# Four layers on one core: where the exponentials of the last layer stand, how its last tiles are read out, and where a flag is loaded

## The chip, the core and the metric

The kernel runs on one core of a Trainium2 chip. A core has five engines with a queue of instructions each, which they work off in order: TensorE (matmul), VectorE, ScalarE, GpSimd and SyncE; in the profile they are PE (with PEld for its weight loads), DVE, ACT, POOL and SP. They wait for each other by semaphores only. Data move between main memory and the on-chip memory by DMA, and TensorE writes into a small memory of its own, PSUM, which VectorE and ScalarE can read. The metric is device time in microseconds. A time is the median of runs without the profiler; one further execution was taken by the hardware profiler, and all views of the trace come from it.

## The reference, cut to what matters

Four layers follow each other on x of shape (4, 512, 32, 32), each as `x = x + layer(groupnorm(x))`. The first three (attention over pixels with mixed heads, a gate, a second attention) are not touched by the change. The last one looks up rows of a pool of 2048 items:

```python
q = jnp.transpose(x, (0, 2, 3, 1)).reshape(-1, C)          # 4096 tokens x 512
att = q @ mempool.T                                         # 4096 x 2048
vals, idx = jax.lax.top_k(att, k)                           # k = 8
vals = jax.nn.softmax(vals, axis=1)
att_sparse = jnp.zeros_like(att).at[rows, idx].set(vals)
out = att_sparse @ mempool                                  # a weighted sum of 8 rows
```

So for each token the eight best of 2048 scores are found, their softmax is taken, and the eight items are added with these weights.

## The kernel before

All lines are of the kernel before. `fast_net` (line 42) computes all four layers; while it does, it keeps sums from which a check can tell whether the softmaxes of the earlier layers, which are taken without a maximum, stayed in range. `check_range` (L2017) turns them into one number, `flag`. `nc.values_load(flag)` puts it into a register of every engine, which is one instruction in each of the five queues, and at the very end the program branches on it to a slower general version (L2788), which isn't run here.

The last layer cuts the 4096 tokens into 32 tiles of 128. For each tile:

- TensorE multiplies the tile's tokens by the pool. Tiles 2 to 29 go in pairs (`two_tiles`, L1568), by a scheme of seven products of half size in the place of eight. A product is four matmuls of 128x128 by 128x512 in float32, which the profile shows as eight instructions of line L1596. The first, second, third and seventh products are copied out of PSUM by ScalarE (L1600); the others are added to scores that are there by VectorE (L1050, `att<-att,pair`). The third, fifth and seventh products go on adding to PSUM in which the first stood, and the fourth to that of the second, so each of these begins after the copy of what stands there. Tiles 0, 1, 30 and 31 are multiplied in the plain way (`attention`, L1522; matmuls L1531, copies L1536), the last one in three parts.
- `pick` (L1609): VectorE finds the eight largest scores (L1620; for the last tile from three partial maxima, L1617 and L1618) and their indices (L1622); GpSimd sends eight indirect DMAs, which gather a row of 512 for each token (L1625); VectorE negates the largest score (L1631), and ScalarE takes the exponentials with their sum (L1634, two instructions). SyncE loads the tile of x that the result is added to (L1636).
- `ready` (L1664): VectorE inverts the sum (L1668) and ScalarE scales the exponentials to weights (L1669). `weigh_rows` (L1671): ScalarE scales the eight gathered rows, one instruction each (L1674). `add_up` (L1677): VectorE adds the rows in a tree of three additions of 1024 and one of 512 (L1050, `got` and `acc`). `turn_back` (L1685): TensorE transposes the sum in four pieces (L1689). `put` (L1692): VectorE adds x (L1695) and SyncE stores the tile (L1696).

The last tiles have a second way: `weigh` (L1639) makes weights on VectorE, `diagonals` (L1644) lets ScalarE write eight diagonal matrices of the weights (L1648), and `read_last` (L1651) lets TensorE multiply the gathered rows by them, 32 matmuls of 128x128 (64 instructions, L1657), so that weighing, adding and transposing are one accumulation in PSUM. Before, tiles 30 and 31 are read in this way, and tile 29 and all ahead of it by the tree.

The order of the work is written out by hand: `pin` keeps an instruction behind everything that was written before it for its engine. What is not pinned, such as the load of the flag, is placed by a scheduler, and what is pinned behind it goes along. The loop at L2049 runs over n = 2, 4, ... 28, one pair of tiles a pass. It draws the seven products out of `two_tiles` one by one and puts between them the picking of tiles n - 1 and n and the weighing, adding, turning and storing of tiles n - 4 to n - 1. In pass n = 12 it calls `check_range`, in pass n = 14 it loads the flag (L2073). Behind the loop, L2108 to L2145 write out the same for the last tiles: s is the tile whose scores are made.

On ScalarE the order in a pass before is: copy of the last pass's seventh product, four rows of n - 3, copy of the first product, four rows of n - 3, exponential of n - 1, copies of the second and third, weights and four rows of n - 2, weights of n - 1, four rows of n - 2, exponential of n. There are three places in PSUM for products, and three buffers for scores.

Of the kernel before, what the change touches and what calls it, by code (L numbers as in the profile page):

```python
# [16 lines left out]
P = 128  # L17
# [14 lines left out]
TOPK = 8  # L32
# [9 lines left out]
def fast_net(ctx: ExitStack, tc: tile.TileContext, a: dict, out: bass.AP, flag: bass.AP):  # L42
# [13 lines left out]
    def pin(ins):  # L56

        return tc.keep_in_program_order(ins)
# [1460 lines left out]

        return eight_k([P, NI], f"att_{n}", at)  # L1520

    def attention(n, between=None, at=None):  # L1522

        b, tt = tiles[n]
        att = new_att(n, at)
        for i, (lo, hi) in enumerate(
                ((0, T), (T, T + NB), (T + NB, NI)) if n == len(tiles) - 1 else ((0, T), (T, NI))):
            sc = flat2(next_pair())
            for i0 in range(lo, hi, NB):
                for k in range(KC):  # L1530
                    pin(nc.tensor.matmul(  # L1531
                        sc[:, i0 - lo:i0 - lo + NB],
                        xn3[b][:, k, tt * P:(tt + 1) * P], memT[k][:, i0:i0 + NB],
                        start=(k == 0), stop=(k == KC - 1),
                    ))
            pin(nc.scalar.copy(att[:, lo:hi], sc[:, 0:hi - lo]))  # L1536
            if between is not None and i == 0:
                between()
        return att

    mem_t = [eT_flat[:, i * NI:(i + 1) * NI].rearrange("p (k q) -> p k q", k=2) for i in range(4)]
# [18 lines left out]
    def token_sums(n):  # L1560

        a11, a12, a21, a22 = token_blocks(n)
        s1, s2, s3, s4 = token_places
        sub7(s3, a11, a21)
        add7(s1, a21, a22)
        sub7(s2, s1, a11)
# [42 lines left out]
    def pick(n, att):  # L1609

        b, tt = tiles[n]
        nm = f"{b}_{tt}"
        top = small.tile([P, TOPK], F32, tag="top", name=f"top_{nm}")
        if n == len(tiles) - 1:
            tops = small.tile([P, 3, TOPK], F32, tag="tops", bufs=1, name="tops")
            for i, (lo, hi) in enumerate(((0, T), (T, T + NB), (T + NB, NI))):
                pin(nc.vector.max(tops[:, i, :], att[:, lo:hi]))  # L1617
            pin(nc.vector.max(top, tops.rearrange("p i n -> p (i n)")))  # L1618
        else:
            pin(nc.vector.max(top, att))  # L1620
        ix = small.tile([P, TOPK], mybir.dt.uint32, tag="ix", name=f"ix_{nm}")
        pin(nc.vector.max_index(ix, top, att))  # L1622
        got = big("qkv"[n % 3], f"got_{nm}").rearrange("p k (i c) -> p (k i) c", c=C)
        for i in range(TOPK):
            pin(nc.gpsimd.indirect_dma_start(  # L1625
                out=got[:, i, :], out_offset=None, in_=a["mem"],
                in_offset=bass.IndirectOffsetOnAxis(ap=ix[:, i:i + 1], axis=0),
                bounds_check=NI - 1, oob_is_err=False,
            ))
        nmx = small.tile([P, 1], F32, tag="nmx", name=f"tmx_{nm}")  # L1630
        pin(nc.vector.tensor_scalar_mul(nmx, top[:, 0:1], -1.0))  # L1631
        et = small.tile([P, TOPK], F32, tag="et", name=f"et_{nm}")
        rs = small.tile([P, 1], F32, tag="rs", name=f"trs_{nm}")
        pin(nc.scalar.activation(et, top, AF.Exp, bias=nmx, scale=1.0, accum_out=rs))  # L1634
        xr = spare[:, n % 4 * NB:(n % 4 + 1) * NB].rearrange("p (k q) -> p k q", q=P)
        nc.sync.dma_start(out=xr, in_=x2[b][:, :, tt * P:(tt + 1) * P])  # L1636
        return got, et, rs, xr

    def weigh(et, rs, nm):  # L1639
        ri = small.tile([P, 1], F32, tag="ri", name=f"tri_{nm}")  # L1640
# [23 lines left out]
    def ready(n, picked):  # L1664

        got, et, rs, xr = picked
        ri = small.tile([P, 1], F32, tag="ri", name=f"tri_{n}")
        pin(nc.vector.reciprocal(ri, rs))  # L1668
        pin(nc.scalar.activation(et, et, AF.Identity, scale=ri))  # L1669

    def weigh_rows(picked, lo, hi):  # L1671
        got, et, rs, xr = picked
        for i in range(lo, hi):
            pin(nc.scalar.activation(  # L1674
                got[:, i, :], got[:, i, :], AF.Identity, scale=et[:, i:i + 1]))
# [272 lines left out]
    for b in range(B):  # L1948
        last = b + 1 == B
        behind = chain(  # L1950
            behind if b else state["behind"], norm3(b - 1) if b > 0 else gating(B - 1))
        ahead = prepare3(0) if last else prepare2(b + 1)
        if last:
            load_memory()
        for s, u in enumerate(UNITS2):
            if s == 5 and not last:
                load2(b + 1)
            if s == 5 and last:
                img[b]["Wp"] = load_w("Wp", f"Wp2_{b}")
            if s >= 1:  # L1960
                scores2(b, u, UNITS2[s - 1], last or u != UNITS2[-1])
            for _ in range(2):
                if s >= 3 and last:
                    next(behind, None)
                if s >= 7:
                    next(ahead, None)
            if s == 9 and b == 0:
                weights = weight_sums(1, "Wq")
            if s >= 10 and b == 0:
                next(weights, None)  # L1970
            if s == len(UNITS2) - 2 and not last:
                run_out(ahead)
                first7, rest7 = input_sums(img[b + 1]["xn"])
                first7[0]()
        run_out(ahead)
        if not last:
            first7[1]()
            first7[2]()
        apply2(b, UNITS2[-1])
        if last:  # L1980
            atts[0] = attention(0, lambda: invert2(b))
            finish2(b)
            put_out2(b, memory_sums())
            continue
        over_keys(b, *UNITS2[-1][:2])
        at_border[0] = True
        for i, _ in enumerate(seven_by_channels(b + 1, "q", bq2)):
            if 1 <= i < 3:
                rest7[i - 1]()
            if i == 4:  # L1990
                invert2(b)
            if i == 5 and b == 0:
                run_out(weight_sums(1, "Wk"))
            if i in (2, 3, 5, 6):
                next(behind, None)
        load_sums(b, "Wp", b == 0)
        for i, _ in enumerate(seven_by_channels(b + 1, "k", bk2)):
            if i == 1:
                finish2(b)
            if b == 0 and i == 2:  # L2000
                run_out(weight_sums(1, "Wv"))
            if b == 0 and i == 4:
                run_out(weight_sums(0, "Wp"))
            next(behind, None)
        first7, rest7 = input_sums(img[b]["o"])
        for i, _ in enumerate(seven_v(b + 1)):
            if 2 <= i < 5:
                first7[i - 2]()
            elif i >= 5:
                rest7[i - 5]()  # L2010
            next(behind, None)
        run_out(behind)
        at_border[0] = False
        scores2(b + 1, UNITS2[0])
        seven_out(b)
# [16 lines left out]

    atts[1] = attention(1)
    picks[0] = pick(0, atts.pop(0))
    token_sums(2)
    att_at[0] = (turns8[0] - 1) % 3
    made = {}

    def add_tile(n):
        made[n] = add_up(n, picks.pop(n))  # L2040

    def turn_tile(n):
        sums[n] = turn_back(n, made.pop(n))

    def put_tile(n):
        put(n, sums.pop(n))

    ahead = iter(())
    for n in range(2, end - 2, 2):  # L2049
# [19 lines left out]
        next(behind, None)  # L2069
        if n == 12:  # L2070
            check_range()
        if n == 14:
            again = nc.values_load(flag, min_val=0, max_val=1)  # L2073
        ready(n - 2, picks[n - 2])
        if n > 2:
            add_tile(n - 3)
# [18 lines left out]

        next(parts)
        atts[n + 1] = next(parts)
        if n + 2 < end - 2:
            token_sums(n + 2)
        if n > 2:  # L2100
# [7 lines left out]
        turn_tile(s - 4)  # L2108
        weigh_rows(picks[s - 3], 4, TOPK)

    atts[s] = attention(s, first_part, (att_at[0] + 1) % 3)
    picks[s - 1] = pick(s - 1, atts.pop(s - 1))
    ready(s - 2, picks[s - 2])
    put_tile(s - 4)
    add_tile(s - 3)
# [1 line left out]

    s = end - 1
    picks[s - 1] = pick(s - 1, atts.pop(s - 1))
    ready(s - 2, picks[s - 2])  # L2120

    def second_part():
        turn_tile(s - 4)
        weigh_rows(picks[s - 2], 0, 4)

    atts[s] = attention(s, second_part, (att_at[0] + 2) % 3)
    put_tile(s - 4)
    weigh(*picks[s - 1][1:3], s - 1)
    add_tile(s - 3)
    weigh_rows(picks[s - 2], 4, TOPK)  # L2130
    diags[0] = diagonals(0, picks[s - 1][1])

    s = end
    picks[s - 1] = pick(s - 1, atts.pop(s - 1))
    turn_tile(s - 4)
    weigh(*picks[s - 1][1:3], s - 1)
    add_tile(s - 3)
    put_tile(s - 4)
    turn_tile(s - 3)
    diags[1] = diagonals(1, picks[s - 1][1])  # L2140
    put_tile(s - 3)
    sums[s - 2] = read_last(picks.pop(s - 2), diags[0])
    sums[s - 1] = read_last(picks.pop(s - 1), diags[1])
    put_tile(s - 2)
    put_tile(s - 1)  # L2145
    return again


# [702 lines left out]
```

## Time and profile before

| | |
|---|---|
| median of 3 runs | 2495.71 us (2493.08 to 2501.78) |
| the profiled execution | 2504.67 us, of which the span of its instructions 2503.0 us |
| TensorE, VectorE, GpSimd, ScalarE busy | 97%, 74%, 49%, 47% of the span |
| mean granted clock of TensorE | 0.994 of full speed |
| last layer's loop, 13 passes from n = 4 | 2082.63 to 2433.74 us |
| one late pass (2366.00 to 2392.73) | 26.73 us: TensorE 25.18 busy, VectorE 24.16, GpSimd 17.19, ScalarE 15.00 |
| behind the loop (2433.74 to 2503.00) | 69.26 us: TensorE 46.49 busy, VectorE 36.91, GpSimd 34.71, ScalarE 25.95 |

How to read the lines of the profile: a row of the timeline gives the start in us from the first instruction, the duration in us, the engine, the line of the kernel, the operation, the tile written and the tiles read, sizes, and how many instructions are merged (x8). In brackets stands how long the engine was idle before it, and whose work ended that idle time; "issue" is a wait that the profile does not explain. Matmuls are pipelined, so a product's row is longer than the distance to the next one's start. A row of the waits gives a total, a count and the longest wait. A q behind the engine's name (ACTq) means its queue: an instruction that only sets or loads registers.

### The profile page before, as it was taken

To read this page: it belongs to the slowest core of one execution; us is meant where nothing else is said; L and a number is where in the kernel's file an instruction comes from. 1 tells how busy PE (TensorE), PEld (TensorE's weight loads), DVE (VectorE), ACT (ScalarE), POOL (GpSimd) and SP (SyncE) were. 2 spreads that over 40 slices of the span, in tenths; PEclk is the share of its full clock that TensorE was granted. 3 is DMA by queue.
4 is the path that set the end of the run, shared out by engine and by line. 5 is a ranking of instruction groups with operands and counts; after the bars stand their busy time and mean duration, and the time that the engine had idled before them with its cause. 6 is when DMAs were issued, how large, how long until landed. Compare 5 with 4: busy or idle time off the path is not lost. (4 is left out here: it accounts for less than half of the span.)

```text
span 2503.0 us, 47967 instructions
## 1 busy us (share of the span) xinstructions
PE 2430.2 (97%) x18400; PEld 1154.5 (46%) x18400; DVE 1847.7 (74%) x2918; ACT 1175.1 (47%) x1516; POOL 1215.8 (49%) x1688
## 2 busy tenths in 40 slices
PE   9999999999999999999999999999999999999996
PEld 4344534555355534555633633453363344444444
DVE  5799568875788548886768677576857657889894
ACT  1567346652666336651253145125324516565653
POOL 3266425553465435554284247127405616666664
PEclk9999999999999999999999999999999999999998
DMA  2588348872698438893301230131114046777765
GB/s 85 154 225 232 118 130 228 241 218 85 176 243 234 140 89 212 244 243 131 103 24 68 104 128 18 64 110 46 55 39 147 26 132 176 230 218 198 200 194 158
DMA packets 190031, 367.18 MB, mean 147 GB/s; under 512 B 32985, under 2 KB 96473, under 8 KB 185570
## 3 DMA queue, kind: packets, MB, share of 16 engines
q1 hardware_dynamic: 109712, 186.58, 23.9%
q0 software_dynamic: 49152, 142.79, 21.2%
q10 hardware_dynamic: 30930, 34.66, 5.1%
q8 instruction: 148, 2.42, 0.4%
q14 instruction: 89, 0.73, 0.1%
HBM read 190.10 MB, written 39.58 MB: 92 GB/s over the span
## 5 line engine op out<-in xcount | busy, mean ns | idle before, releaser
L552 DVE STREAM_TRANSPOSE eT<-e 128x1024 f32<-128x1024 f32 x256 | 316.6, 1237 | 197.1 <-ACT e L546 196.5
L528 POOL DMA_DIRECT2D s<-ss x512 | 258.2, 512 | 386.4 <-PE pair L539 110.5
L1365 ACT ACTIVATE eT<-pair 128x1024 f32<-128x1024 f32 x256 | 248.2, 1022 | 312.4 <-PE pair L1371 189.1
L1625 POOL DMA_INDIRECT got<-in_mem,ix x256 | 277.1, 1082 | 202.7 <-issue 68.8
L567 DVE BATCH_NORM_STATS2 st<-e 128x6 f32<-128x256 f32 x1024 | 350.8, 405 | 0.0
L546 ACT ACTIVATE e<-pair 128x1024 f32<-128x1024 f32 x256 | 250.4, 1022 | 161.7 <-PE pair L539 129.9
L1389 POOL TENSOR_TENSOR e<-eT 128x1024 f32<-128x1024 f32 x96 | 239.3, 2496 | 167.0 <-ACT eT L1365 122.0
L519 ACT COPY ss<-pair 128x1024 f32<-128x1024 f32 x256 | 247.2, 1020 | 83.7 <-PE pair L513 41.7
L513 PE MATMUL pair<-k,q 64*32 64x512 f32 x4096 | 267.3, 598 | 11.5 <-ACT e L546 11.5
L578 PEld LDWEIGHTS pv<-eT,v 128*64 128x64 f32 x4096 | 221.1, 137 | 71.6 <-issue 55.2
L578 PE MATMUL pv<-eT,v 128*64 128x128 f32 x4096 | 250.0, 275 | 4.0 <-ACT pv L638 4.0
L1371 PE MATMUL pair<-q,k 64*128 64x512 f32 x1024 | 239.9, 605 | 1.8 <-DVE sum L1050 0.9
L1390 DVE TENSOR_TENSOR eT<-eT,e 128x1024 f32<-128x1024 f32 x96 | 146.9, 1530 | 126.7 <-POOL e L1389 126.4
L1596 PE MATMUL pair<-eT,tokens 128*128 128x512 f32 x448 | 201.3, 592 | 0.0
L539 PE MATMUL pair<-s,wmix 32*32 32x512 f32 x4096 | 160.0, 599 | 3.0 <-DMA s<-ss 2.1
L1385 POOL TENSOR_TENSOR eT<-eT 128x1024 f32<-128x1024 f32 x32 | 83.0, 2593 | 161.4 <-ACT eT L1365 156.1
L1371 PEld LDWEIGHTS pair<-q,k 64*128 64x128 f32 x1024 | 92.3, 186 | 140.0 <-issue 66.6
L1674 ACT ACTIVATE got<-got,et 128x512 f32<-128x512 f32 x240 | 153.2, 711 | 1.4 <-DMA got<-in_mem,ix 1.0
L513 PEld LDWEIGHTS pair<-k,q 64*32 64x32 f32 x4096 | 57.1, 105 | 178.5 <-ACT e L546 85.4
L1050 DVE TENSOR_TENSOR k<-k,pair 128x512 f32<-128x512 f32 (+1 forms) x96 | 78.0, 857 | 73.6 <-PE pair L1123 60.5
L1596 PEld LDWEIGHTS pair<-eT,tokens 128*128 128x128 f32 x448 | 84.1, 190 | 100.9 <-issue 98.1
L651 POOL TENSOR_TENSOR o<-pv,rb 64x256 f32<-64x256 f32 x128 | 118.7, 927 | 6.3
(410 smaller groups left out, 3706.3 us busy)
## 6 DMA issues: line engine op xcount, KB each, us to landing
s<-ss SPq DMA_DIRECT2D x512, 128.0 KB
s<-ss POOLq DMA_DIRECT2D x512, 128.0 KB
rb<-r POOLq DMA_DIRECT2D x64, 128.0 KB
o<-o SPq DMA_DIRECT2D x32, 256.0 KB
xr_c<-x SPq DMA_DIRECT2D x32, 256.0 KB
rb_c<-r SPq DMA_DIRECT2D x64, 128.0 KB
e<-x SPq DMA_DIRECT2D x32, 256.0 KB
out<-e SPq DMA_DIRECT2D x32, 256.0 KB
```

The costliest lines, as they stand in the source:

```text
L513: pin(nc.tensor.matmul(sc[m * NS:(m + 1) * NS, r, :], q[r * HD:(r + 1) * HD, m, s * NS:(s + 1) * NS], k_[r * HD:(r + 1) * HD, m, n * NB:(n ...
L519: pin(nc.scalar.copy(ss[:, :, n * NB:(n + 1) * NB], sc))
L528: pin(relays[side].dma_start(out=s2[2 * m + r::NH], in_=ss[m * NS:(m + 1) * NS, r, :]))
L546: pin(nc.scalar.activation(e[:, half].rearrange("p r qq k -> p (r qq k)"), flat2(mixed(s, half)), AF.Exp))
L552: pin(nc.vector.transpose(eT[:, j % 2].rearrange("p b (qq i r) x -> p i r qq b x", qq=2, i=4)[:, i, 2 * half:2 * half + 2], e[:, half].rea ...
L567: pin(nc.vector.bn_stats(st[:, i, 2 * half + r, qq, :], e[:, half, r, qq, :]))
L578: pin(nc.tensor.matmul(pv[r * HD:(r + 1) * HD, gp, :], I["v"][:, t, g * HD:(g + 1) * HD], eT[:, j % 2, t, :, 4 * g:4 * g + 4], start=(t == ...
L1365: pin(nc.scalar.activation(e, scs[len(es)], AF.Exp, scale=SCALE))
L1371: pin(nc.tensor.matmul(sc[:, r, :], I["k"][r * HD:(r + 1) * HD, m, t * P:(t + 1) * P], I["q"][r * HD:(r + 1) * HD, m, n * NB:(n + 1) * NB] ...
L1389: nc.gpsimd.tensor_add(two, es[i], es[i + 1])
L1596: pin(nc.tensor.matmul(ps[:, c, :], a_[:, k, :], b_(k, c), start=(start and k == 0), stop=(k == 1), skip_group_check=True))
L1625: pin(nc.gpsimd.indirect_dma_start(out=got[:, i, :], out_offset=None, in_=a["mem"], in_offset=bass.IndirectOffsetOnAxis(ap=ix[:, i:i + 1], ...
```

## The change

In the loop, `pick` no longer writes the exponential itself. It leaves it with `soften(n)`, which the loop calls for tile n - 1 behind the copies of the second and third products, and for tile n behind the copy of the seventh. For the last tile the negation stands ahead of the search for indices. The load of the flag moves from pass 14 to the end, behind the transposes of tile 28. Tile 29 is read by diagonals too, so three tiles are; their diagonals for 29 and 30 are written between the parts of the last tile's scores. The tree of tile 28 stands ahead of the addition of tile 27's x (`put_tile`) on VectorE. The diff without the moved closing lines of `pick`:

```diff
+        nmx = small.tile([P, 1], F32, tag="nmx", name=f"tmx_{nm}")
+        if n == len(tiles) - 1:
+            pin(nc.vector.tensor_scalar_mul(nmx, top[:, 0:1], -1.0))
         ix = small.tile([P, TOPK], mybir.dt.uint32, tag="ix", name=f"ix_{nm}")
         pin(nc.vector.max_index(ix, top, att))
...
-        pin(nc.scalar.activation(et, top, AF.Exp, bias=nmx, scale=1.0, accum_out=rs))
         xr = spare[:, n % 4 * NB:(n % 4 + 1) * NB].rearrange("p (k q) -> p k q", q=P)
         nc.sync.dma_start(out=xr, in_=x2[b][:, :, tt * P:(tt + 1) * P])
+        soft[n] = lambda: pin(
+            nc.scalar.activation(et, top, AF.Exp, bias=nmx, scale=1.0, accum_out=rs))
         return got, et, rs, xr
...
+    def soften(n):
+        soft.pop(n)()
...
         if n == 12:
             check_range()
-        if n == 14:
-            again = nc.values_load(flag, min_val=0, max_val=1)
+        soften(n - 1)
         ready(n - 2, picks[n - 2])
...
         atts[n + 1] = next(parts)
+        soften(n)
...
     s = end - 1
     picks[s - 1] = pick(s - 1, atts.pop(s - 1))
-    ready(s - 2, picks[s - 2])
+    weights(s - 2)
+    add_tile(s - 3)
 
     def second_part():
         turn_tile(s - 4)
-        weigh_rows(picks[s - 2], 0, 4)
-
-    atts[s] = attention(s, second_part, (att_at[0] + 2) % 3)
-    put_tile(s - 4)
-    weigh(*picks[s - 1][1:3], s - 1)
-    add_tile(s - 3)
-    weigh_rows(picks[s - 2], 4, TOPK)
-    diags[0] = diagonals(0, picks[s - 1][1])
+        soften(s - 1)
+        diags[0] = diagonals(0, picks[s - 2][1])
+
+    def third_part():
+        put_tile(s - 4)
+        weights(s - 1)
+        diags[1] = diagonals(1, picks[s - 1][1])
+
+    atts[s] = attention(s, (second_part, third_part), (att_at[0] + 2) % 3)
 
     s = end
     picks[s - 1] = pick(s - 1, atts.pop(s - 1))
+    soften(s - 1)
     turn_tile(s - 4)
-    weigh(*picks[s - 1][1:3], s - 1)
-    add_tile(s - 3)
+    again = nc.values_load(flag, min_val=0, max_val=1)
     put_tile(s - 4)
-    turn_tile(s - 3)
-    diags[1] = diagonals(1, picks[s - 1][1])
-    put_tile(s - 3)
-    sums[s - 2] = read_last(picks.pop(s - 2), diags[0])
-    sums[s - 1] = read_last(picks.pop(s - 1), diags[1])
-    put_tile(s - 2)
-    put_tile(s - 1)
+    weights(s - 1)
+    diags[2] = diagonals(2, picks[s - 1][1])
+    for i in range(3):
+        sums[s - 3 + i] = read_last(picks.pop(s - 3 + i), diags[i])
+        put_tile(s - 3 + i)
     return again
```

`weights(n)` calls `weigh` for tile n. `attention` now takes several such functions and calls one behind each part's copy.

## The prediction

> **What bounds the kernel now.** I read the share of busy time first: TensorE 97% of a span of 2503.0 us, so time is lost only where TensorE stands still, and what is gained must come from those places. Then I asked for TensorE's own waits in the stretch that the change touches, 2060 us to the end:
>
> ```profile
> engine line waited for: us in total, times, longest us
> PE pair L1596 <- ACT att L1600: 21.2, 13, 2.9
> PE pt L1689 <- DVE acc L1050: 13.0, 1, 13.0
> PE pv L1689 <- issue: 2.8, 1, 2.8
> ```
>
> There are two losses: 13 short waits, one in each pass of the loop over pairs of tiles from n = 4 on, and about 16 us at the end. The timeline of one pass says what the short wait is (start, duration, engine, line). TensorE, the first four of its seven products of 8 instructions:
>
> ```profile
> 2380.28 3.60 PE L1596 MATMUL pair<-memT,eT 128*128 128x512 f32 x8
> 2383.71 3.60 PE L1596 MATMUL pair<-eT,tokens 128*128 128x512 f32 x8
> 2387.58 3.60 PE L1596 MATMUL pair<-eT,tokens 128*128 128x512 f32 x8
> 2392.73 3.70 PE L1596 MATMUL pair<-eT 128*128 128x512 f32 x8 [1.55 <-ACT att L1600]
> ```
>
> ScalarE in the same stretch:
>
> ```profile
> 2384.82 2.56 ACT L1674 ACTIVATE got<-got,et 128x512 f32<-128x512 f32 x4
> 2391.39 0.30 ACT L1634 ACTIVATE et<-top,tmx 128x8 f32<-128x8 f32 x1 [4.01 <-issue]
> 2391.60 0.19 ACT L1634 ACTIVATION_READ_ACCUMULATOR et<-top,tmx 128x1 f32 x1
> 2391.69 1.91 ACT L1600 COPY att<-pair 128x1024 f32<-128x1024 f32 x2
> ```
>
> VectorE:
>
> ```profile
> 2389.02 2.29 DVE L1622 FIND_INDEX8 ix<-top,att 128x8 uint32<-128x2048 f32 x1
> 2391.22 0.13 DVE L1631 TENSOR_SCALAR tmx<-top 128x1 f32<-128x1 f32 x1
> ```
>
> The fourth product adds to PSUM that the second product wrote, so it needs the copy of the second (the copy at 2391.69). That copy could have run from 2387.3, but it stands on ScalarE behind the exponential of the tile being picked, which waits for the negated maximum, and that stands on VectorE behind the search for indices. ScalarE sits idle for 4.01 us with the copy in its queue. The end of the span I read last, TensorE:
>
> ```profile
> 2465.03 0.66 PE L1689 MATMUL pv<-ident,acc 128*128 128x128 f32 x4 [2.78 <-issue]
> 2478.72 1.11 PE L1689 MATMUL pt<-ident,acc 128*128 128x128 f32 x4 [13.04 <-DVE acc L1050]
> 2479.62 9.28 PE L1657 MATMUL pv<-eT,got 128*128 128x128 f32 x64
> 2488.74 7.31 PE L1657 MATMUL pt<-eT,got 128*128 128x128 f32 x64
> ```
>
> ScalarE, the last two copies of scores:
>
> ```profile
> 2466.74 0.59 ACT L1536 COPY att<-pair 128x512 f32<-128x512 f32 x1 [8.27 <-PE pv L1689]
> 2468.22 0.58 ACT L1536 COPY att<-pair 128x512 f32<-128x512 f32 x1 [0.89 <-remote]
> ```
>
> The last scores are done at 2462.1, and TensorE then waits for VectorE's tree of tile 29 (acc at 2478.7) before it may read out tiles 30 and 31.
>
> **The exponentials.** Nothing is added in a pass: two exponentials move. The built order of the changed kernel agrees with the one of before on VectorE, GpSimd and SyncE through the ordinary passes, and on ScalarE both exponentials stand behind the copies. The second product's copy there waits for one thing of VectorE, the addition into that tile's buffer in the pass before, long done. Working through a pass from its first product (0): products take 3.43 us each start to start, the two sets of transposes 0.44, so 7 x 3.43 + 2 x 0.44 = 24.9 us without a wait, against 26.73 (2380.28 to 2407.01): 1.83 us a pass, the 1.55 that the wait shows and the slow restart. What is late next? ScalarE: copy at 0.2, exponential 0.4, four rows 2.46, copy, four rows, copy of the second product at 7.3 to 8.2; TensorE wants it at 10.7. The moved exponential runs at 11.8 (behind the copy of the third product), and the first who asks for its sum is VectorE's reciprocal at 19.0, so 6.8 us of cover. The other one (behind the last copy) ends at 1.5 and is asked for at 11.1. GpSimd's gathers follow the indices, not the exponential (the last index to the first gather is 0.76 us in each pass), and each block of eight takes 10.5 to 11.0 us where 12.2 and 12.7 are left. VectorE is nearest: 24.16 us busy of 26.73 and idle for 2.33 only while it waits for products four and five. Without the stall it adds product five at 17.8 and is free at 17.2: 0.6 us of slack. TensorE stays the bound, narrowly.
>
> **The flag out of the loop.** The register load at n = 14 stands in the built order with the reciprocal and the scaling pulled ahead, so that in this pass eight rows (one of them waiting for its gather until 2226.2) stand before the copies. The pass takes 30.40 us (2216.23 to 2246.63), 5.5 more than 24.9: a longer wait (2.88), 0.6 at the transposes, and a product that takes 5.23 instead of 3.43 because the clock was granted at half for 3.4 us after the wait. In the changed order this pass is like the others. Sum for the loop: 13 passes took 351.1 us (2082.63 to 2433.74); 13 x 24.9 plus 0.3 for two small products that now cost is 324.0. **Gain 27 us**, 22 by the twelve ordinary passes.
>
> The flag is still loaded by each engine, on three of them now at the end (on GpSimd and SyncE it keeps its place). The trace shows it:
>
> ```profile
> L2073 PEldq TENSOR_LOAD <-flag x1: 486/486/486, 2223.7 to 2223.7; - x1
> L2073 ACTq TENSOR_LOAD <-flag x1: 490/490/490, 2216.6 to 2216.6; - x1
> ```
>
> On ScalarE it stands between the last exponential and the last diagonals, which wait 2 us more for their weights; on VectorE ahead of an addition that waits for TensorE; on TensorE between the transposes of tile 28 and the first read-out, the only place where it could show. At 2223.7 it ran while products were queued and nothing was late, so its cost lies between 0 and 0.5 us; I take 0.3. The Trainium skill speaks against such a load: Runtime: NRT & Kernel Launch, section "The ~15µs preamble/postamble breakdown", gives the register loads at launch about 1.3 us. By that the end would lose 1.3 on TensorE; the row, 0.49, is for this very load, and I keep it.
>
> **The end.** Count from E, the first product of tile 30 (2433.74 now, about 2406.7 after). Scores and two sets of transposes end at E + 28.4, as now. ScalarE: first copy of tile 31 at 21.2 to 22.1, exponential of 30, eight diagonals for tile 29 (2.4 us now) to 24.9, second copy 25.1 to 25.7, diagonals for 30 to 28.1, third copy 28.6 to 29.1. VectorE: weights of 29 at 20.2 (in place of a scaling on ScalarE), tree of 28 (3.6 and 0.65) to 24.7 ahead of the addition that now waits from 2453.9 to 2459.6, so the transposes of 28 no longer wait. The diagonals for 30 are a new wait ahead of the third copy: they need the weights of 30 (25.7), end at 28.1, and the product of that copy ends at 28.4, so 0.3 us of cover; what they exceed it by delays the last maximum. VectorE goes on with two maxima, an addition at 29.0 that waits for these transposes (it holds the last maximum back by 0.45), last maximum 29.6, negation, indices to 33.2, gather from 34.0 to 45.0, its last row in by 48 if it lands in 3 us. TensorE reads out 29, 30 and 31 from 28.8 + 0.3, each 7.16 us warm (2488.90 to 2496.06): to E + 50.6. The last row of 31 is wanted at 49.7, so the gather stays just hidden. What is removed is the tree of 29 (4.4 us VectorE) with its eight scalings and its transposes from the path; what is added, 7.16 us of TensorE, lies in its 13 us of idle time.
>
> Here a rule of the skill decides 2 us: TensorE: Matmul & The Clock Gate, "Part 1: The HAM clock gate", says that the array falls to half clock after an idle window of some 3.4 us. The row agrees for now (granted 0.53 from 2466 to 2479, and the first read-out takes 9.07 us, 1.9 more). After, TensorE has no gap over 0.5 us before the read-outs, so I take 7.16 for all three; were it cold, the end would come 1.9 us later.
>
> From the last product to the span's end is 6.9 us now and after: E + 57.5 against E + 69.3. **Gain 11.8 us by this trace.** But in it the copy at 2466.74 comes 8 us after its product ended at 2458.7, with ScalarE idle, and no row explains it. Played without that delay, the end of before is at about E + 63.4 and the gain 5.9; these are the two bounds. The profiled execution took 2504.67 us (the span and 1.67 around it), 9.0 above the median of 2495.71. The section of the Runtime page named above puts some 6 us between a profile's total and the reported time, which no run here shows; that leaves 3 us of the delay for the profile alone, so I take 11.8 - 3 = 9. Sum: 27 + 9 = 36; from 2504.67 that gives 2468.7 for a profiled execution, and from the median **2459.7, so 2460 us**.
>
> **Rivals.** (1) VectorE becomes the bound: its 0.6 us of slack goes to waits of its own. For: 24.16 us busy in a pass of 24.9. Against: its order is unchanged and its waits on TensorE fall with the stall. At 25.8 us a pass the loop gains 15, in all 24: 2472. (2) The end doesn't gain: the unexplained late signals come again at the new end and the gather of tile 31 sets it; 6 us late, its last row lands at 54, the end is at E + 62, and against E + 63.4 that is 1.4 us of gain, in all 28: 2467. (3) The change doesn't do what it says: the copy of the second product waits for something else as late as the exponential. The built order speaks against it; only the end and n = 14 would gain: 2483. (4) Slower: the sum of the moved exponential comes so late that VectorE's reciprocal, with the maximum and the indices behind it, waits for it, and TensorE waits for VectorE. It starts beyond 6.8 us of delay, costs 13 times each further us, and ends the whole gain at 9.6 us: with 10 us late, about 2501. The exponential takes 0.4 us and waits for nothing later than 11.8, so I give it little.
>
> **Chances.** Forecast 0.77; (1) 0.10; (2) 0.07; (3) 0.03; (4) 0.03. The forecast runs from 27 + 11.8 (2457) to 27 + 5.9 (2463), and 3 us more on each side for the spread of the runs (2493 to 2502). To 2453 below; above, (2) is inside, and (1) with part of the loop's gain reaches 2470. About 0.3% (7.5 us) is what a measurement can tell from no change: faster 0.95, same 0.03, slower 0.02.
>
> **What would show it.** The waits of TensorE on the copies at L1600 fall from 21.2 us to under 2; pass to pass 24.9 to 25.0, n = 14 too; no half clock near 2230 or before the read-outs; three read-outs of 7.2 us without a gap; the last copies within 0.3 us of their products. It is wrong if TensorE waits in each pass for an acc or att of VectorE (rival 1), if the last read-out waits for its gather (rival 2), or if the pass stays at 26.7.

## The result, and the profile after

| | before | after |
|---|---|---|
| median (4 runs each) | 2495.78 us (2493.08 to 2501.78) | 2466.61 us (2464.59 to 2468.99) |
| profiled execution | 2504.67 us | 2464.59 us |
| 13 passes from n = 4 to tile 30's first product | 351.1 us | 324.3 us |
| from that product to the end of the span | 69.3 us | 57.6 us |

The ratio is 0.988, with a 95% interval of 0.986 to 0.990: 29 us less, or 25 to 35. Forecast were 36 us less and a time of 2460 us. The loop and the end of the changed kernel are counted from these products on TensorE, the first of pass n = 4 and the first of tile 30; the span is 2462.9 us:

```profile
2080.98 3.60 PE L1596 MATMUL pair<-memT,xn_d 128*128 128x512 f32 x8
...
2405.28 1.88 PE L1531 MATMUL pair<-memT,eT 128*128 128x512 f32 x4
```

Then TensorE's waits of the changed kernel, from 2050 to 2470 us. The answer has a heading and no row: the 21.2 us behind the copies, the 13.0 us for the tree and the 2.8 us are all gone.

```profile
core 0 of [0], span 2462.9 us
engine line waited for: us in total, times, longest us
```

The timeline of a pass shows the products on TensorE without a gap. From the first product of one pass to that of the next it is 2380.37 - 2355.46 = 24.91 us, where it was 26.73.

```profile
2355.46 3.60 PE L1596 MATMUL pair<-memT,eT 128*128 128x512 f32 x8
2358.89 3.60 PE L1596 MATMUL pair<-eT,tokens 128*128 128x512 f32 x8
...
2366.20 3.60 PE L1596 MATMUL pair<-eT 128*128 128x512 f32 x8
...
2380.37 1.02 PE L1596 MATMUL pair<-memT,eT 128*128 128x512 f32 x2
```

ScalarE in that pass: the copy of the second product (2362.67) runs as soon as the product is done, three and a half microseconds ahead of the fourth product (2366.20), and the exponential (2367.31) stands behind the third copy.

```profile
2362.67 0.99 ACT L1600 COPY att<-pair 128x1024 f32<-128x1024 f32 x1
2366.40 1.01 ACT L1600 COPY att<-pair 128x1024 f32<-128x1024 f32 x1 [2.74 <-PE pair L1596]
2367.31 0.30 ACT L1640 ACTIVATE et<-top,tmx 128x8 f32<-128x8 f32 x1
```

VectorE is the engine with the least room. In this pass it waits once, for the fifth product:

```profile
2373.26 1.22 DVE L1050 TENSOR_TENSOR att<-att,pair 128x1024 f32<-128x1024 f32 x1 [0.60 <-PE pair L1596]
```

At the end TensorE goes from the transposes of tile 28 through three read-outs without a gap and at full clock (granted 1.00 from 2405 to 2455.6), and ScalarE copies the last scores within 0.1 us of their products' ends:

```profile
2433.63 0.60 PE L1698 MATMUL pv<-ident,acc 128*128 128x128 f32 x4
2434.06 7.31 PE L1666 MATMUL pt<-eT,got 128*128 128x128 f32 x64
2441.21 7.31 PE L1666 MATMUL pv<-eT,got 128*128 128x128 f32 x64
2448.36 7.31 PE L1666 MATMUL pt<-eT,got 128*128 128x128 f32 x64
```

```profile
2430.39 0.59 ACT L1536 COPY att<-pair 128x512 f32<-128x512 f32 x1 [0.23 <-PE pair L1531]
2433.83 0.59 ACT L1536 COPY att<-pair 128x512 f32<-128x512 f32 x1 [0.33 <-PE pair L1531]
```

Loop and end fit what the forecast read from the trace to half a microsecond (324.0 and 57.5), and yet the trace cannot be read as it stands. By the spans the gain is 40 us; by the medians it is 29. The profiled execution of before lay 8.9 us above its median, that of after 2.0 below. The experiments had to say which microseconds of the old end were real.

### The profile page after: what moved, and what is told of

The parts are those of the page before. It is cut to its first block, busy times and chain, and to the rows that moved or that the text cites. A ratio compares the mean times of both kernels' runs of the same rounds, so it can differ in the third digit from the quotient of the medians.

```text
span 2462.9 us, 48090 instructions
## 1 busy us (share of the span) xinstructions
PE 2429.7 (99%) x18460; PEld 1158.8 (47%) x18460; DVE 1841.6 (75%) x2915; ACT 1170.2 (48%) x1515; POOL 1217.2 (49%) x1688
## 4 chain that ended last, share of the span: by engine, by line
PE 89%; DVE 4%; ACT 3%; DMA 2%; issue 1%; POOL 1%; SPq 0%; ACTq 0%; POOLq 0%
PE pair L1596 14%; PE pair L1123 13%; PE pv L578 9%; PE pair L1371 8%; PE pair L513 7%; PE pair L199 6%; PE pair L539 6%; PE pt L471 5%; PE pt L1408 4%; PE pv L1408 4%; PE pair L1249 4%; PE pt L767 4%; PE pair L1531 2%; ACT e L546 2%; DMA s<-ss 1%
## 5 line engine op out<-in xcount | busy, mean ns | idle before, releaser
L1683 ACT ACTIVATE got<-got,et 128x512 f32<-128x512 f32 x232 | 148.0, 710 | 0.5
```

## Experiments: the parts one by one

"The old end" is the code behind the loop of before, "the new end" that of after; an end is measured from tile 30's first product. Each time is compared with runs of before taken beside it, since before itself read 2495.8, 2504.4, 2506.8, 2497.8 and 2498.5 us in the five sets of runs. The last four sets ran on four different chips: 13 (the first four rows), 3 (the next four), 4 (cut_before, b_nog30) and 11 (the last two); the chip of the first set is not known. A difference between sets can therefore be one between chips.

| kernel | median, us | before beside it | ratio (95% interval) | end in its profile, us |
|---|---|---|---|---|
| b_again | 2504.28 | 2504.4 | 0.9999 (0.9988 to 1.0009) | 69.6 |
| exp_only | 2478.92 | 2504.4 | 0.9896 (0.9881 to 0.9911) | 68.9 |
| flag_only | 2500.42 | 2504.4 | 0.9985 (0.9978 to 0.9991) | 69.1 |
| end_only | 2498.05 | 2504.4 | 0.9976 (0.9968 to 0.9984) | 61.3 |
| after_again | 2474.94 | 2506.83 | 0.9876 (0.9856 to 0.9895) | 64.1 |
| exp_flag | 2480.35 | 2506.83 | 0.9889 (0.9874 to 0.9903) | 70.5 |
| dve_069 | 2473.95 | 2506.83 | 0.9860 (0.9845 to 0.9875) | 67.2 |
| dve_229 | 2494.45 | 2506.83 | 0.9947 (0.9934 to 0.9959) | 67.4 |
| cut_before | 2450.38 | 2497.8 | 0.9812 (0.9798 to 0.9825) | cut off |
| b_nog30 | 2497.1 | 2497.8 | 0.9998 (0.9988 to 1.0008) | 61.7 |
| b_nog30_2 | 2500.02 (one run) | 2498.46 | - | 62.0 |
| exp_late | 2505.27 | 2498.46 | 1.0023 (1.0014 to 1.0032) | 56.8 |

**b_again**: no edit.

> The kernel before, profiled a second time; nothing is edited. Theory A (the late copies of the last scores belong to that one profiled execution): here the last two copies at L1536 begin 0.2 to 0.3 us after their products end, the end stands about 63.4 us behind the first product of tile 30 in place of 69.3, the span is near 2494 and the profiled execution within 3 us of the median of about 2496. Theory B (they come in every run of this code): the copies are 6 to 8 us late again, the end is 69 us behind tile 30's first product, and the span is near 2503 again. Both expect the passes of 26.73 us and the pass n = 14 of 30.4 us to come again.

The end was 69.6 us long again, so theory A's "one execution" falls. ScalarE's last copies in this profile, and TensorE's products that they copy:

```profile
2449.70 1.88 PE L1531 MATMUL pair<-eT 128*128 128x512 f32 x4
...
2453.58 1.88 PE L1531 MATMUL pair<-eT 128*128 128x512 f32 x4
...
2457.01 1.88 PE L1531 MATMUL pair<-eT 128*128 128x512 f32 x4
```

```profile
2454.14 1.01 ACT L1536 COPY att<-pair 128x1024 f32<-128x1024 f32 x1 [2.37 <-issue]
2464.71 1.07 ACT L1536 COPY att<-pair 128x512 f32<-128x512 f32 x2 [7.11 <-remote]
```

The three products end at about 2451.5, 2455.4 and 2458.9; the copies begin 2.6, 9 and 6 us later. (The two last copies are one row.) I call such copies, which begin long after their product with ScalarE idle, late signals of TensorE. Yet the profiled execution took 2501.71 us, below the median of its set.

**exp_only**: `soften` as in the change; the flag in pass 14 and the old end stay.

```diff
+        soften(n - 1)
         ready(n - 2, picks[n - 2])
...
         atts[n + 1] = next(parts)
+        soften(n)
```

> Only the exponentials of the loop stand behind the copies; the flag is loaded in pass n = 14 and the end is that of before. Theory A: ordinary passes of 24.9 us, so 22 us less from twelve of them. Pass n = 14: by the prediction's accounting (the register load itself shuffles the order, 3.7 of its 5.5 us) it stays at 28 to 29 us, the gain is 23 to 24, the time about 2472. Rival to that accounting: on ScalarE the load now stands behind the copies, so pass 14 takes about 25 too, the whole 27 comes from the exponentials, time about 2469, and moving the flag as well adds nothing. Theory B (the loop gives less in ordinary runs than in the trace, since the end gives its full 11.8 of the 29.2): a gain of about 17, time 2479.

25.5 us less (22 to 30). The profile settles pass 14 (TensorE, its first product and that of the next pass): 25.60 us with the load of the flag still in it.

```profile
2208.18 3.60 PE L1596 MATMUL pair<-memT,eT 128*128 128x512 f32 x8
2211.61 3.60 PE L1596 MATMUL pair<-eT,tokens 128*128 128x512 f32 x8
2215.68 0.66 PE L1695 MATMUL pv<-ident,acc 128*128 128x128 f32 x4 [0.48 <-DVE acc L1050]
...
2233.78 1.45 PE L1596 MATMUL pair<-memT,xn_d 128*128 128x512 f32 x3
```

So the load was not what made pass 14 slow by itself. With the exponential gone from the place ahead of the copies, the scheduler's shuffle costs 0.7 us.

**flag_only**: the load behind the transposes of tile 28, nothing else.

```diff
-        if n == 14:
-            again = nc.values_load(flag, min_val=0, max_val=1)
...
     turn_tile(s - 4)
+    again = nc.values_load(flag, min_val=0, max_val=1)
```

> Only the load of the flag goes from pass n = 14 to the end, behind the transposes of tile 28; exponentials and end are those of before. All theories: pass 14 becomes an ordinary one of 26.73 us in place of 30.40, a gain of 3.7 us, time about 2492. If the load were not the cause of that pass's order it would stay at 30.4 and the time at 2496. At the end the load lies in TensorE's wait for the tree of tile 29: 0.

4.0 us less (2.3 to 5.5), pass 14 takes 26.72 us, and the waits in the loop keep their number but lose their long one (1.6 in place of 2.9 us):

```profile
engine line waited for: us in total, times, longest us
PE pair L1596 <- ACT att L1600: 19.8, 13, 1.6
```

**end_only**: the changed kernel with the loop of before.

```diff
         picks[n - 1] = pick(n - 1, atts.pop(n - 1))
+        soften(n - 1)
...
-        soften(n - 1)
+        if n == 14:
+            again = nc.values_load(flag, min_val=0, max_val=1)
         ready(n - 2, picks[n - 2])
...
         picks[n] = pick(n, atts.pop(n))
+        soften(n)
...
-        soften(n)
...
-    again = nc.values_load(flag, min_val=0, max_val=1)
```

> Only the end is changed (tile 29 by diagonals too, the tree of 28 ahead of the addition, the last exponentials between the parts of tile 31's scores); in the loop the exponentials stand in their old place ahead of the copies and the flag is loaded in pass n = 14. Theory A (late copies in one profile only): a gain of 2 to 6 us, time 2490 to 2494. Theory B (late in every run): a gain of about 11.8, time 2484. Both: the end stands 57.5 us behind tile 30's first product, with three read-outs of 7.2 us without a gap.

6.4 us less (4.0 to 8.0). Here late copies came with the new end too, and TensorE paused inside the read-outs; the end was 61.3 us long, not 57.5.

**after_again** (no edit to the changed kernel) and **exp_flag** (the edits of exp_only and flag_only together: all of the change but the end):

> The changed kernel, measured again beside more runs of the kernel before. If the parts add up as they did one by one (25.5 by the exponentials alone, about 6.4 by the end alone, nothing more by the flag, whose pass already took 25.6 us in the run with the exponentials alone): 32 us of gain, a ratio of 0.987. If the end gives its full 11.8 only together with the others: 37 us, 0.985. If it gives next to nothing with them: 27, 0.989. In the profile: no late copies at the end (as in the first profile of this kernel), or late ones here too, as in the run with the new end alone; then they come and go by themselves.

> The loop of the changed kernel (exponentials moved, no flag in it), the flag at the end, and the old end of before: all of the change but the end. Against the run with the exponentials alone this moves only the flag: pass 14 goes from 25.6 us to 24.9, so the gain over before is 26 us and not 27 + 3.7. Against the changed kernel it lacks only the end: it should be 6 us slower by the one-by-one runs, 11.8 slower by the prediction's upper bound. In the profile the last copies of scores are 2 to 8 us late again, as in all four profiles of the old end.

The changed kernel gained 31.9 us, exp_flag 26.5, so by the medians of four runs each the end is worth 5.4 in its place; the intervals of the two ratios overlap, so that it could be nothing or twice as much. The loop with the flag gives 26.5 where the traces of before and after say 26.8 (375.4 to 348.6 us for the 14 passes). Exp_flag's own passes took 349.8: in pass n = 4 TensorE waits 1.1 us for a tree, and in after_again it waits there for 1.4 us, in dve_069 too; the first profile of the changed kernel has no such wait. What the flag adds to the exponentials is too little for the timed runs to tell (26.5 against 25.5, in two sets); the traces say 0.7 us and not 3.7, since the two edits heal the same pass. The new end of after_again took 64.1 us. Its rows on TensorE show how:

```profile
2437.01 1.95 PE L1666 MATMUL pt<-eT,got 128*128 128x128 f32 x16
2439.22 0.27 PE L1666 MATMUL pt<-eT,got 128*128 128x128 f32 x1 [0.26 <-issue]
2440.61 0.38 PE L1666 MATMUL pt<-eT,got 128*128 128x128 f32 x2 [1.13 <-issue]
2442.02 0.27 PE L1666 MATMUL pt<-eT,got 128*128 128x128 f32 x1 [1.02 <-issue]
2442.72 5.08 PE L1666 MATMUL pt<-eT,got 128*128 128x128 f32 x44 [0.43 <-issue]
```

```profile
2441.33 0.58 ACT L1536 COPY att<-pair 128x512 f32<-128x512 f32 x1 [7.82 <-issue]
```

From 2438.7 to 2442.7 TensorE moves by one matmul or less each 0.7 us, waiting for nothing that the profile shows, and the copy of scores that were done at 2433.3 begins at 2441.33, 8 us late. Late signals and the halting read-out come in the same microseconds, so I take them for one disturbance.

## Experiments: is the disturbance in the timed runs?

**cut_before**: before, with everything behind the loop taken out.

```diff
             put_tile(n - 3)
-    s = end - 2
-    weigh_rows(picks[s - 3], 0, 4)
...
-    put_tile(s - 1)
     return again
```

> The kernel before, cut off behind the loop: the scores of tiles 30 and 31 and the output of the last tiles are left out. It measures how long the end of before takes in the timed runs: the time of before less the time of this kernel, plus this kernel's own short end from its profile. Theory A (the late signals at the end of before are in the profile alone): 63.4 us. Theory B (they are in the timed runs too): 69.4, as in all five profiles of the old end (68.9 to 70.5). In the profile: if late signals belong to whatever stands last in the program, the last two passes of this kernel show them too (TensorE's signals over 1 us late); if they belong to the stage of tile 31, they are gone.

The timed difference is 47.4 us (43.7 to 50.5). This kernel's last product begins at

```profile
2430.15 3.60 PE L1596 MATMUL pair<-eT,tokens 128*128 128x512 f32 x8
```

and the next would have begun 3.43 us later, 14.3 us ahead of the end of its span (2447.9). So the old end takes 61.7 us (58.0 to 64.8) in this set's timed runs: theory A's side, not 69.4. Its last two passes show no late signal (TensorE waits twice, 3.1 us in all, for the copies, as in before), so late signals don't belong to whatever stands last.

**b_nog30** and **b_nog30_2** (the same kernel, profiled twice):

```diff
-        for i in range(TOPK):
+        for i in range(TOPK if n != len(tiles) - 2 else 1):
             pin(nc.gpsimd.indirect_dma_start(
...
+        if n == len(tiles) - 2:
+            pin(nc.gpsimd.memset(got[:, 1:TOPK, :], 0.0))
```

> The kernel before, with seven of the eight gathers of tile 30 left out (GpSimd fills these rows with zeros instead; the output of that tile differs). The late signals of the old end begin 17 to 25 us behind the first product of tile 30, where these gathers start (20.9). If the gathers' traffic makes them late: the last copies begin within 0.5 us of their products and the end stands at about 63 us behind that product. If not: 69 again.

> The kernel before with seven of the eight gathers of tile 30 left out, profiled once more. If it is the gathers that make TensorE's signals late at the end of a profiled execution, they are on time again and the end stands 61 to 62 us behind tile 30's first product, as in the first profile of this kernel. If that one was chance: 69, as in the five profiles of the old end with all gathers.

Both profiles show an undisturbed old end, 61.7 and 62.0 us. In the first, the last products, the transposes and the first read-out on TensorE, and the last copies on ScalarE:

```profile
2457.39 1.88 PE L1531 MATMUL pair<-eT 128*128 128x512 f32 x4
...
2460.83 1.88 PE L1531 MATMUL pair<-eT 128*128 128x512 f32 x4
2462.54 0.60 PE L1691 MATMUL pv<-ident,acc 128*128 128x128 f32 x4
2473.24 1.11 PE L1691 MATMUL pt<-ident,acc 128*128 128x128 f32 x4 [10.10 <-DVE acc L1050]
2474.15 9.10 PE L1659 MATMUL pv<-eT,got 128*128 128x128 f32 x64
```

```profile
2459.31 0.59 ACT L1536 COPY att<-pair 128x512 f32<-128x512 f32 x1 [0.37 <-PE pair L1531]
2462.74 0.59 ACT L1536 COPY att<-pair 128x512 f32<-128x512 f32 x1 [2.85 <-PE pair L1531]
```

The wait of 10.10 us is what the undisturbed old end costs, and with it about 1.8 us of the read-out behind it, a row of 9.10 in place of 7.31: TensorE stands for the tree of tile 29 and for no late signal. The medians of b_nog30 and of before lie 0.7 us apart, so in this set before mostly ran without the disturbance. Single runs reach 2504.64 (b_nog30) and 2503.33 us (before).

A sum shows how the five sets could differ. A time is the start of the loop (2055 to 2061 us in thirteen profiles, 2065 in exp_late; I take 2058.5), 375.3 for the 14 passes, the end, and 1.8 around the span. With an end of 61.8 that gives 2497.4 us for before: the sets that read 2495.8, 2497.8 and 2498.5. With 69.4 it gives 2505.0: the sets of 2504.4 and 2506.8. For after, with 349 for the passes, it gives 2466.9 with its end of 57.6 (measured 2466.61), and 2474.3 with 65, the mean of the four disturbed new ends of the table (61.3, 64.1, 67.2, 67.4; measured 2474.94). So neither theory holds as I put it. By this estimate the disturbance is in the timed runs of two sets, and in the first set in the profiled execution of before, not in most of its timed runs. That is not shown: the start of the loop alone varies by as much as the two ends differ, cut_before was measured in an undisturbed set only, and two slower chips would give the same times. In the profiles the disturbance lengthens both ends, the old by 7.6 us and the new by 4 to 10. So the gain of the end is 4.2 us undisturbed (61.8 to 57.6), and disturbed 4.4 by the profiles (69.4 to 65) and 5.4 and 6.4 by the timed runs.

## Experiments: the covers of the loop

**dve_069** and **dve_229**: one more VectorE instruction in a pass of the changed kernel (dve_229 takes all 2048 columns).

```diff
+    extra = small.tile([P, TOPK], F32, tag="extra", bufs=1, name="extra")
...
             add_tile(n - 3)
+            pin(nc.vector.max(extra, memT[0][:, 0:512]))
```

> The changed kernel with one more VectorE instruction in each pass, a maximum over 512 constants (0.69 us) ahead of the addition of the fifth product. The prediction gave VectorE 0.6 us of slack there, 0.75 us idle in the whole pass: the instruction takes the place of the idle time, passes stay at 24.9 to 25.0, the time within 2 us of the changed kernel. If VectorE already bounded the pass (rival 1): 13 x 0.7 = 9 us slower.

> The same with a maximum over 2048 constants (2.29 us). VectorE then has 24.16 + 2.29 = 26.45 us of work in a pass and becomes the bound: passes of 26.4 to 26.5, 1.55 x 13 = 20 us slower than the changed kernel, and TensorE waits for VectorE's tiles in each pass. If the slack were larger than read (waits of VectorE elsewhere that could move), less: 10 or so.

dve_069 is no slower than after_again (2473.95 against 2474.94, either good to 4 or 5 us, where rival 1 asked for 9); the late passes stay at 24.91 us. dve_229 is 19.5 us slower, with passes of 26.4, and TensorE's waits up to tile 30 name VectorE:

```profile
PE pv L1698 <- DVE acc L1050: 8.2, 7, 1.3
PE pt L1698 <- DVE acc L1050: 4.6, 4, 1.3
PE pt L1698 <- DVE e L1704: 1.7, 1, 1.7
```

**exp_late**: the exponential of tile n - 1 later on ScalarE than its cover allows.

```diff
-        soften(n - 1)
         ready(n - 2, picks[n - 2])
...
+        weigh_rows(picks[n - 2], 4, TOPK)
+        if n > 2:
+            row = picks[n - 2][0][:, TOPK - 1, :]
+            for _ in range(6):
+                pin(nc.scalar.activation(row, row, AF.Identity, scale=1.0))
+        soften(n - 1)
         ready(n - 1, picks[n - 1])
-        weigh_rows(picks[n - 2], 4, TOPK)
```

> The changed kernel with the moved exponential of tile n - 1 put later still: on ScalarE behind all eight rows of n - 2 and six more instructions of a row's size (a row copied to itself, about 0.62 us each). It then starts some 17.1 + 3.8 us into the pass and its sum is there at about 21.4, where VectorE's reciprocal asks for it at 19.0: 2.4 us beyond the cover of 6.8. The prediction's price is 13 times each us beyond, less the 0.6 to 0.75 us that VectorE idles in a pass: 13 x 1.7 = 22 us slower than the changed kernel, passes of 26.6 us. If the cover is larger than read, or VectorE takes the delay without TensorE waiting: 0.

In the late passes VectorE's reciprocal waits 2.45 us for the exponential, as worked out, and TensorE for VectorE's tree (one late pass of VectorE, then TensorE's waits up to tile 30):

```profile
2391.60 1.22 DVE L1050 TENSOR_TENSOR att<-att,pair 128x1024 f32<-128x1024 f32 x1 [0.27 <-PE pair L1596]
2395.28 0.16 DVE L1677 RECIPROCAL tri<-trs 128x1 f32<-128x1 f32 x1 [2.45 <-ACT et L1640]
```

```profile
PE pv L1698 <- DVE acc L1050: 17.2, 8, 2.4
PE pt L1698 <- DVE acc L1050: 6.6, 3, 2.4
PE pair L1596 <- DVE tokens L1050: 3.1, 6, 1.2
```

But it costs more than 22 us. Against before it is 1.0023 where the changed kernel is 0.9876, so 1.0149 of the changed kernel: 37 us (36 with the 0.988 of the first set). The trace shows why. VectorE's waits for the exponential in the 13 passes (2089 to 2453 us):

```profile
DVE tri L1677 <- ACT et L1640: 39.4, 13, 4.4
```

Seven of them are 2.45 us and the passes take 27.05 us late in the loop. The other six are 3.4 to 4.4 us, in passes in which ScalarE also scales a part of the next image (L1509, 1.23 us) between the rows and the exponential; the longest pass takes 30.6 us. All 13 passes took 363.6 us, 39.3 more than in the changed kernel: the 39.4 us of waiting passed on in full. VectorE's idle time took up 0.3 us in a late pass (its wait for the fifth product is 0.27 where it was 0.60), not the 0.6 to 0.75 that I had counted on, and nothing in the sum.

## Why the prediction was right, and what was mis-sized

- **What bounds the kernel** held: ScalarE's copy behind the exponential. Moving the exponentials alone took all 13 waits away, and the ordinary passes came to 24.91 us (24.9 forecast); 25.5 us of gain in the timed runs. With the flag it is 26.8 us in the trace (27) and 26.5 in the timed runs of exp_flag.
- **Pass 14**: its time was right, its cause was split wrongly. I gave 22 us to the twelve ordinary passes and put the 5.5 of this one under the flag. With the exponentials moved and the load left, the pass took 25.60 us, which is 4.8 of the 5.5; with only the load moved 26.72, which is 3.7 of them. The price belonged to the load and the exponential together: the load's shuffle put more work ahead of a copy that waited already.
- **The covers** held where they were narrow. VectorE waits 0.60 us for the fifth product (0.6 forecast): 0.69 us more in a pass cost nothing, 2.29 cost 19.5 (20). The cover of 6.8 us on ScalarE was right to 0.1 us in passes that prepare no image. The price on record, 13 times each further us, held as well: 39.4 us of waiting made 39.3 in the trace and 37 in the timed runs; my expectation of 22 counted on VectorE's idle time and left out the work for the next image.
- **The flag at the end** cost nothing on TensorE (0.3 taken). Its queue runs ahead of the array: the load stands behind the transposes of tile 28 (2433.63) and ran 3.5 us before them, while products of tile 31 were still running:

  ```profile
  L2153 PEldq TENSOR_LOAD <-flag x1: 483/483/483, 2430.1 to 2430.1; - x1
  ```

- **The end** is the step that failed in size: "that leaves 3 us of the delay for the profile alone, so I take 11.8 - 3 = 9". It is worth 4.2 us in undisturbed profiles, and in the two sets in which it was timed 6.4 (4.0 to 8.0) and 5.4 (with overlapping intervals). My bound of 11.8 set a disturbed old end against an undisturbed new one. The lower bound of 5.9 was nearer, and even it was 1.7 too high: I played the undisturbed old end to 63.4 us, and it is 61.7. The 3 us came from the Trainium skill (Runtime: NRT & Kernel Launch, "The ~15µs preamble/postamble breakdown"), which puts some 6 us between a profile's total and the execution time that the runtime reports. I used that for another distance, the one of a single execution from the median of others, and this is no fixed amount in these runs: the profiled executions lay 2.0 (after) and 2.6 us (b_again) below their medians, 2.9 (flag_only) and 8.9 (before) above. The distance that the page means no run here shows. Without the 6 us, the 9 us of before would have covered the whole delay of 5.9, and the end would have stood at the lower bound.
- **The sum**: 26.8 + 4.2 = 31 us, with the measured 29 (25 to 35) and 31.9 us around it. I said 36, and most of what is too much is the end's. The range holds 2466.6 only through the allowance for rivals: the forecast proper, 2457 to 2463 with 3 us on each side, just misses it.
- **The rivals.** Rival (2), with 2467, named the measured number better than the forecast did, but not by its cause: in the first profile the last read-out waits for nothing. Much of it came true in other sets, where four of six new ends had late signals: in after_again the gathers of tile 31 start 41.3 us behind tile 30's first product (34.3 in the first profile) and their traffic ends at about 54, as the rival says. Whether the last read-out halts for them there is open, since the profile puts all its waits to "issue". Rival (1) fell with dve_069, (3) with the waits at L1600, which are all gone, and (4) came at the price it named once exp_late brought its condition about.

Open stays what the disturbance is. That the gathers of tile 30 belong to it is not shown. Two profiles without them are clean and all five of the old end with them are not, but those two come from chips 4 and 11, on which no old end with all gathers was profiled, and on 11 the new end was clean with all its gathers (exp_late); and the gathers of 28 other tiles make no signal late. Whether it goes with the chip, with the loads of instructions or with the profiler was not tested; before, b_nog30 and cut_before on one chip that shows it would tell. Whether the timed runs of one set mix both kinds was not settled either: before spread over 7.6 us and b_nog30 over 10 where cut_before's five runs lay within 0.8.

## What to carry to other kernels

An instruction that waits in a queue holds up everything behind it, so ask of each wait on a copying engine whether the copy behind it was ready, and move the waiting instruction behind the copy. When two edits cure the same stall, price them together and alone: here either edit took 4.8 or 3.7 us from one pass, and both together 5.5. And before a stage's length in one profile is set against its length in another, look for a delay that no row explains, and count the stage without it on both sides. How much of it is real is asked of timed runs, as by leaving the stage out; the distance of one execution from the median doesn't say, since b_again lay 2.6 us below its median with an end of 69.6.

## What was not expected of the hardware

In the last 50 us of nine executions work that waits for TensorE began 2 to 11 us after its product had ended, while the products themselves ran on at 3.43 us a product; in the new end TensorE was then held to about one matmul each 0.7 us. Of six profiles of the new end two were free of it (57.6 and 56.8 us), four not (61.3, 64.1, 67.2 and 67.4). The clock of TensorE fell to half in each old end, where it stood still for about 9 us and more (before: granted 0.51 from 2474 to 2484), and the row of the read-out behind that wait took 8.4 to 9.3 us in place of 7.3; the undisturbed new end had no such gap and kept 1.00.
